# Routed expert blocks: one table built after the last batch, or three tables built after two, three and four batches

## The chip, the cores and the metric

The kernel runs as one program on one core of one Trainium2 chip. The metric is device time in microseconds (us) of one execution; less is better. The core has a matrix engine (PE, with its weight loads PEld), a vector engine (DVE), a scalar engine (ACT), a general engine (POOL), and a queue engine (SP) which here only issues DMAs. Each engine runs its own instructions in a fixed order; engines wait for each other by semaphores.

## The reference, cut to what matters

The input x is 4 batches of 512 tokens of 256 numbers, all fp32. Four layers follow each other. Each adds an attention over a small context (64 keys a batch; layer 1 has a causal self-attention, MLA, besides) and then a feed-forward part. In layers 0, 1 and 3 this part is a mixture of experts, of which each token takes two:

```python
scores = jnp.einsum('btd,de->bte', x, router_w)
probs = softmax(scores)                                   # layer 1: sigmoid
routing_weights, routing_idx = jax.lax.top_k(probs, 2)
routing_weights = routing_weights / jnp.sum(routing_weights, axis=-1, keepdims=True)
gate = einsum(x, gate_proj[expert]);  up = einsum(x, up_proj[expert])
expert_out = (silu(gate) * up) @ down_proj[expert]
y = sum over the two chosen experts of routing_weight * expert_out
...
# layer 1: shared = silu(xt @ Wg_s) * (xt @ Wu_s) @ Wd_s is added for every token
```

Layer 0 has 8 experts with a hidden width of 704, layer 1 has 7 of 256 and a shared one, layer 3 has 8 of 512. Layer 2's feed-forward part is dense (FP4 quantized) and plays no part here. The two snippets are shortened: the reference computes all experts and weights them, the kernel only the chosen ones.

## The kernel before

**Tokens and batches.** x stays on the core as 16 tiles of 128 tokens. A batch `g` (0 to 3) is four tiles. Attention runs batch by batch; as soon as a batch has its attention result, its tokens are routed, while PE works on the next batch.

**Routing a batch** is `route` (L1054) in layers 0 and 3 and the second half of `mla_after` (L1260) in layer 1. Its steps: layer norm (statistics on DVE, a square root on ACT, `ln_rs` and `ln_sh` on DVE L337, the normalized rows `xn` on ACT L340), transposes (`ps_xT` L372), the router's scores (`r_lg`), `top2` (L731: two maxima, then weights through an exp), then `Routed.add` (L817). `add` marks the chosen experts (`e_mk`, `e_pm`), has PE count each token's rank within its expert (`ps_rank` L829 and L830, then `e_rank`), and writes each token's row, with its place and weights, into its expert's region of a DRAM tensor `xs` by eight indirect DMAs from POOL (L842). The regions hold 2048 rows an expert and are zero where nothing was written.

**The table.** Only after the last batch does `add` call `table` (L854 to L885). From the counts of all four batches (`ps_cnt` L858) it lists blocks of 128 rows, expert by expert: for each block its expert and its first row in `xs`, as integers in `e_tab`. The number of blocks is fixed at the worst case, `nb` = 39 (8 experts) or 38 (7 experts).

**The blocks.** `blocks` (L1005) walks the table. SP reads an entry into a register (`value`) and issues the loads that depend on it: `weights(b)` (L913) loads the expert's gate and up matrices `e_wgu` (three buffers) and its down matrix `e_wd` (four), three blocks ahead; `tokens(b)` (L925) loads 128 rows `e_x` (five buffers), five blocks ahead. For each block `up` (L933) transposes the rows (`ps_xe` L939, copied to `e_xT` L942 or L945 by DVE), works out the places and weights (`places` L896, small DVE operations), multiplies (`ps_gu` L953), takes silu on ACT (`e_s` L969) and multiplies gate by up on DVE (`e_h` L970). `turn` (L973) transposes the block before (`ps_he` L982, evacuated to `e_hT`), `down` (L990) multiplies it (`ps_de` L995), weights it on ACT (`e_y` L997) and scatters it from POOL into `ys` (L998). The next layer adds the rows of `ys` to x. The heart of the loop:

```python
for b in range(self.nb):
    now = self.up(b, between)          # between() calls turn for the block before
    if last:
        self.down(turned, *last)
    last = now
    next(other, None)                  # a piece of the next layer's preparation, layer 0 only
    self.weights(b + 3)
    self.tokens(b + 5)
```

**What sets the order.** Each engine's order is fixed when the program is built. Attention runs under `in_order(PE)`: PE's order is as the program writes it, and a list scheduler places the rest. Blocks run under `in_order(DVE, SP)`: DVE and SP as written, PE, ACT and POOL by the scheduler. In `xattn` (L632), the attention of layers 0, 1 and 3, generators interleave batches: `new` prepares the next batch, `old` (`rest`) finishes the one before (products `ps_bc`, `ps_cy` L592 and `cy`, projection `ps_p` L607, addition to x, then `after`, which is `route`), and the current one runs its scores and exponentials (`ctx_weights` L544: `ps_cx` L552, `cpr` L558 on ACT). The MLA loop (L1290) walks steps `t` (row maxima `mq` L1147 of `ps_ms`, weights `mpr` from `ps_mx` L1157, sums `ps_mo` L1180) and gives each a piece of `mla_after` of an older batch. `mla_after` starts with `mla_project` (`ps_mn`, `my`, `ps_myT`, `myT`, `ps_mw`, addition to `xl`), then a second norm, scores, `add` and `shared_expert` (L757: `ps_sg` L766, `ps_su`, `ps_sd`). For the last batch a pipelined `mla_project_last` (L1220 to L1258) takes the place of `mla_project`.

**The seams.** At the end of attention in layer 0 (seam 1 in what follows), of the MLA in layer 1 (seam 2) and of attention in layer 3 (seam 3), the last batch has nothing behind it to interleave with.

Of the kernel before, what the change touches and what calls it, by code (L numbers as in the profile page):

```python
# [22 lines left out]
P = 128  # L23
B, S, E = 4, 512, 256
SC = 64
# [163 lines left out]
class Net:  # L189
# [136 lines left out]
    def layernorm(self, g, out):  # L326

# [7 lines left out]
        nc.scalar.activation(sd, mv[:, :, 1], AF.Sqrt, bias=self.eps)  # L335
        rs, sh = self.sm("ln_rs", [P, GT]), self.sm("ln_sh", [P, GT])
# [295 lines left out]
    def xattn(self, query, values, scale, dv, W, bias, before=None, after=None, keys=None):  # L632
# [4 lines left out]
        with self.room("xattn") as pool, self.banks(mm=4, sc=1), ExitStack() as stack:  # L637
# [14 lines left out]
            def rest(st):  # L652
                yield from self.ctx_values(pool, st, dv, W)
                if after:
                    yield from after(st.g)
# [13 lines left out]
            for st in sts:  # L669
# [14 lines left out]
                some(late)  # L684
                self.ctx_weights(pool, st, 0, scale)
# [10 lines left out]
            some(old, nf + 2)  # L696
            some(late)
            some(old)
# [32 lines left out]
    def top2(self, v, n, below, logits, rows):  # L731

        nc = self.nc
# [6 lines left out]
        if logits:  # L740
            d, e = self.sm("t_d", [P, GT]), self.sm("t_e", [P, GT])
            nc.vector.tensor_tensor(d, m2, m1, ALU.subtract)
            nc.scalar.activation(e, d, AF.Exp)
            nc.vector.tensor_scalar(s, e, 1.0, None, ALU.add)
            nc.vector.reciprocal(wt[:, :, 0], s)
            nc.vector.tensor_tensor(wt[:, :, 1], e, wt[:, :, 0], ALU.mult)
        else:
            r = self.sm("t_r", [P, GT])
            nc.vector.tensor_tensor(s, m1, m2, ALU.add)
            nc.vector.reciprocal(r, s)  # L750
            nc.vector.tensor_tensor(wt[:, :, 0], m1, r, ALU.mult)
            nc.vector.tensor_tensor(wt[:, :, 1], m2, r, ALU.mult)
        return oh1, oh2
# [32 lines left out]
class Routed:  # L786
# [7 lines left out]

    def __init__(self, net, n, F, gu, d, name, stamp, w=None):
        self.net, self.nc, self.n, self.F, self.w = net, net.nc, n, F, w
        self.nf = (F + P - 1) // P
        self.nb = (2 * NT * P + n * (P - 1)) // P
        self.dram_gu, self.dram_d, self.name, self.stamp = gu, d, name, stamp
        self.scattered, self.put, self.loaded = [], [], {}  # L800
        self.run = self.keep("run_", [P, n])
        self.nc.vector.memset(self.run, 0.0)
# [14 lines left out]
    def add(self, g, rows, oh1, oh2):  # L817
# [4 lines left out]
        nc.vector.tensor_copy(pm[:, 0], self.run)  # L822
        for i in range(1, GT):
            nc.vector.tensor_tensor(pm[:, i], pm[:, i - 1], mk[:, i - 1], ALU.add)
        run = self.keep(f"run{g}", [P, n])
        nc.vector.tensor_tensor(run, pm[:, GT - 1], mk[:, GT - 1], ALU.add)
        self.run = run
        ps = net.acc.tile([P, GT, n], F32, tag="acc", name="ps_rank")
        nc.tensor.matmul(ps, net.cst[:, C_LT : C_LT + P], mk, start=True, stop=False)  # L829
        nc.tensor.matmul(ps, net.cst[:, C_ONE : C_ONE + P], pm, start=False, stop=True)  # L830
        rank = net.sm("e_rank", [P, GT, n])
# [19 lines left out]
        if g == B - 1:  # L851
            self.table()

    def table(self):  # L854

        nc, net, n, nb = self.nc, self.net, self.n, self.nb
        ps = net.acc.tile([P, n], F32, tag="acc", name="ps_cnt")
        nc.tensor.matmul(ps, net.cst[:, C_ONE : C_ONE + P], self.run, start=True, stop=True)  # L858
        up, b = net.keep_i("e_up", [P, n]), net.keep_i("e_b", [P, n])
        nc.vector.tensor_scalar(up, ps, float(P - 1), None, ALU.add)  # L860
        nc.vector.tensor_scalar(b, up, 7, None, ALU.logical_shift_right)
        nbf, cum = net.sm("e_nbf", [P, n]), net.sm("e_cum", [P, n])
        nc.vector.tensor_copy(nbf, b)
        nc.vector.tensor_tensor_scan(cum, net.cst[:, C_ONE : C_ONE + n], nbf, 0.0, ALU.mult, ALU.add)
        iota = net.cst[:, C_IOTA : C_IOTA + nb]
        m = n - 1
        wide = [P, nb, m]
        le = self.keep("e_le", wide)
        cb = cum[:, None, :m].to_broadcast(wide)
        nc.vector.tensor_tensor(le, cb, iota[:, :, None].to_broadcast(wide), ALU.is_le)  # L870
        eb, fb, j = net.sm("e_eb", [P, nb]), net.sm("e_fb", [P, nb]), net.sm("e_j", [P, nb])
        nc.vector.tensor_reduce(eb, le, AX.X, ALU.add)
        nc.vector.tensor_tensor(le, le, cb, ALU.mult)
        nc.vector.tensor_reduce(fb, le, AX.X, ALU.max)
        nc.vector.tensor_tensor(j, iota, fb, ALU.subtract)


        nc.vector.tensor_scalar(j, j, float(CAP // P), float(P), ALU.min, ALU.mult)
        tab = self.keep("e_tab", [P, 2, nb], I32)
        nc.vector.tensor_copy(tab[:, 0], eb)  # L880
        nc.vector.scalar_tensor_tensor(tab[:, 1], eb, float(CAP), j, ALU.mult, ALU.add)

        self.eb = self.keep("e_ebs", [P, nb])
        nc.vector.tensor_scalar(self.eb, eb, -float(SC), None, ALU.add)
        self.tab = tab[:1]  # L885

    def value(self, tab, engine, top):
# [5 lines left out]
            skip_runtime_bounds_check_because="the table counts comparisons with n - 1 sums, and clamps the row",  # L893
        )

    def places(self, xb, b):  # L896
# [3 lines left out]
        one, eb = xb[:, R_ONE : R_ONE + 1], self.eb[:, b : b + 1]  # L900
# [12 lines left out]
    def weights(self, b):  # L913
# [3 lines left out]
        pool, sync = self.pool, self.nc.sync  # L917
        es = self.value(self.tab[:, 0, b : b + 1], SP, self.n - 1)
# [86 lines left out]
    def blocks(self, pool, other=()):  # L1005
# [8 lines left out]
        for b in range(3):  # L1014
            self.tokens(b)
# [689 lines left out]
```

## Time and profile before

| | |
|---|---|
| time, median of 3 runs | 2027.19 us (2026.67 to 2031.56) |
| the profiled execution | 2026.92 us |
| its span, first to last instruction | 2025.2 us |
| its mean granted TensorE clock | 0.919 of full speed |
| busy: PE, DVE, ACT, POOL | 1719.9, 974.2, 667.5, 423.5 us |
| DMA: moved, mean rate over the span | 271.59 MB, 134 GB/s |
| one load of `e_wgu`: layer 0, 3, 1 | 1408 KB in 6.1 us, 1024 KB in 5.1, 512 KB in 4.1 |
| one load of `e_x` | 130 KB in 4.8 us |

The busy rows are sums over the whole span. A sum cannot tell where an engine waited, so the page's 40 slices come next, and then stretches of the trace given by start and end in us from the span's start. In a timeline, a row is: start, duration, engine, line, operation, output and inputs, shapes, count, and in brackets how long the engine was idle before it and what ended the wait.

### The profile page before, as it was taken

The numbers are of one execution on the slowest core, as the hardware profiler recorded it, in microseconds if no ns is written. First come the engines' busy times: TensorE is split into PE (matmuls) and PEld (weight loads), VectorE is DVE, ScalarE is ACT, GpSimd is POOL, SyncE is SP. The second block draws the span as 40 slices with busy tenths as digits, with TensorE's granted clock in tenths as the row PEclk, the third lists the DMA queues.
The fourth block names the chain that finished last, engine by engine and source line by source line (L and its number), as shares of the span: only waits on it lengthen the run. The fifth ranks groups of instructions, "written<-read, shape, count | busy, mean of one in ns | idle before, by whom it ended". The sixth has DMA issues, their size and how long they took to land.

```text
span 2025.2 us, 25644 instructions
## 1 busy us (share of the span) xinstructions
PE 1719.9 (85%) x8740; PEld 980.1 (48%) x8740; DVE 974.2 (48%) x2778; ACT 667.5 (33%) x1253; POOL 423.5 (21%) x594
## 2 busy tenths in 40 slices
PE   6875999999869878898999979985998887599994
PEld 3433666666535333343444344444665443355662
DVE  3543344444454334444454335446899454333333
ACT  3431322222253332336343422233455343122221
POOL 2123011111150011122231222223113112311112
PEclk8986999999979988999999889995899898699997
DMA  9615887778320000000000018772000001598995
GB/s 294 180 38 203 319 294 282 288 284 285 133 71 1 16 23 1 1 1 22 1 22 1 22 42 302 265 246 83 1 0 1 12 6 37 186 311 301 302 315 171
DMA packets 109347, 271.59 MB, mean 134 GB/s; under 512 B 13408, under 2 KB 71200, under 8 KB 99104
## 3 DMA queue, kind: packets, MB, share of 16 engines
q1 hardware_dynamic: 82976, 227.97, 33.0%
q0 software_dynamic: 10176, 28.00, 3.7%
q10 hardware_dynamic: 16064, 13.98, 2.1%
q8 instruction: 70, 1.15, 0.2%
q14 instruction: 61, 0.50, 0.1%
HBM read 220.48 MB, written 49.42 MB: 133 GB/s over the span
## 4 chain that ended last, share of the span: by engine, by line
PE 64%; DVE 14%; ACT 5%; issue 3%; POOL 3%; DMA 2%; SPq 0%; ACTq 0%; DVEq 0%; POOLq 0%
PE ps_gu L953 20%; PE ps_de L995 9%; PE ps_ms L1142 4%; PE ps_mo L1180 3%; DVE mq L1147 2%; PE ps_he L982 2%; PE ps_mx L1157 2%; PE ps_f L1564 2%; PE ps_p L607 2%; POOL xs L842 2%; PE ps_bc L586 1%; PE ps_ms L1145 1%; PE ps_xe L939 1%; PE ps_xT L372 1%; PE ps_cy L592 1%
## 5 line engine op out<-in xcount | busy, mean ns | idle before, releaser
L953 PE MATMUL ps_gu<-e_wgu,e_xT 128*128 128x352 f32 (+1 forms) x1088 | 417.7, 524 | 4.4 <-DVE e_xT L945 0.8
L953 PEld LDWEIGHTS ps_gu<-e_wgu,e_xT 128*128 128x128 f32 x1088 | 197.2, 191 | 143.3 <-issue 73.6
L995 PE MATMUL ps_de<-e_wd,e_hT 128*128 128x256 f32 x932 | 232.3, 385 | 3.8 <-ACT e_hT L303 1.5
L970 DVE TENSOR_TENSOR e_h<-e_s,ps_gu 128x352 f32<-128x352 f32 (+2 forms) x155 | 83.5, 539 | 295.0 <-PE ps_gu L953 227.0
L998 POOL DMA_INDIRECT ys<-e_y,e_to x116 | 112.9, 973 | 521.1 <-ACT e_y L997 398.2
L995 PEld LDWEIGHTS ps_de<-e_wd,e_hT 128*128 128x128 f32 x932 | 172.1, 189 | 79.5 <-issue 41.8
L969 ACT ACTIVATE e_s<-ps_gu 128x352 f32<-128x352 f32 (+2 forms) x155 | 74.1, 478 | 326.6 <-PE ps_gu L953 326.6
L1147 DVE TENSOR_REDUCE mq<-ps_ms 128x2 f32<-128x256 f32 (+3 forms) x128 | 105.7, 826 | 139.8 <-PE ps_ms L1145 139.5
L997 ACT ACTIVATE e_y<-ps_de,e_wt 128x256 f32<-128x256 f32 x116 | 55.0, 475 | 259.5 <-PE ps_de L995 248.2
L1159 ACT ACTIVATE mpr<-ps_mx 128x1024 f32<-128x1024 f32 (+3 forms) x128 | 90.1, 704 | 140.1 <-PE ps_mx L1157 136.1
L1142 PE MATMUL ps_ms<-mkT,mqT 32*128 32x512 f32 (+3 forms) x512 | 112.5, 518 | 22.3 <-DVE mq L1147 21.2
L842 POOL DMA_INDIRECT xs<-xn,e_at x96 | 94.1, 981 | 135.2 <-DVE ln_rs L337 75.7
L1157 PE MATMUL ps_mx<-mqm,mkT 32*128 32x128 f32 (+3 forms) x512 | 107.6, 497 | 1.1 <-ACT mpr L1159 1.1
L1161 POOL TENSOR_SCALAR_AFFINE_SELECT mpr<-mpr 128x256 f32<-128x256 f32 x128 | 52.0, 409 | 242.3 <-ACT mpr L1159 242.3
L1180 PE MATMUL ps_mo<-mpr,va 128*32 128x128 f32 (+3 forms) x512 | 96.9, 460 | 3.1 <-POOL mpr L1161 3.1
L1564 PE MATMUL ps_f<-w,xqT 128*128 128x352 f32 x256 | 86.4, 480 | 1.2 <-ACT xqT L1555 1.2
L372 PE MATMUL ps_xT<-consts_sb,xn 128*128 128x128 f32 x256 | 51.8, 341 | 41.8 <-ACT xn L340 27.0
L982 PE MATMUL ps_he<-consts_sb,e_h 128*128 128x128 f32 x466 | 76.2, 278 | 12.0 <-DVE e_h L970 7.9
L939 PE MATMUL ps_xe<-consts_sb,e_x 128*128 128x128 f32 x232 | 51.4, 292 | 37.0 <-DMA e_x<-xs 34.1
L942 DVE COPY e_xT<-ps_xe 128x256 f32<-128x256 f32 x78 | 33.0, 423 | 98.4 <-PE ps_xe L939 98.4
L1142 PEld LDWEIGHTS ps_ms<-mkT,mqT 32*128 32x128 f32 x512 | 41.4, 197 | 77.6 <-DVE mq L1147 52.6
L552 PE MATMUL ps_cx<-q,kbd 32*128 32x512 f32 x256 | 44.0, 786 | 39.5 <-ACT cpr L558 39.5
(314 smaller groups left out, 2776.8 us busy)
## 6 DMA issues: line engine op xcount, KB each, us to landing
e_wgu<-in_e0gu SPq DMA_DIRECT2D x39, 1408.0 KB, 6.1
e_wgu<-in_e3gu SPq DMA_DIRECT2D x39, 1024.0 KB, 5.1
e_wd<-in_e0d SPq DMA_DIRECT2D x39, 768.0 KB, 5.7
e_wd<-in_e3d SPq DMA_DIRECT2D x39, 512.0 KB, 5.4
e_wgu<-in_e1gu SPq DMA_DIRECT2D x38, 512.0 KB, 4.1
xs<-z SPq DMA_DIRECT2D x16, 1040.0 KB, 14.3
e_x<-xs SPq DMA_DIRECT2D x116, 130.0 KB, 4.8
e_wd<-in_e1d SPq DMA_DIRECT2D x38, 256.0 KB, 4.2
```

Source lines behind the costliest of these rows:

```text
L842: r = nc.gpsimd.indirect_dma_start(out=net.xs, out_offset=bass.IndirectOffsetOnAxis(ap=at[:, k, i : i + 1], axis=0), in_=rows[:, i], in_of ...
L953: nc.tensor.matmul(ps[:, :n], xT[:, c], wgu[:, c, cols], start=(c == 0), stop=(c == NC - 1))
L970: nc.vector.tensor_tensor(h[:, k * H : (k + 1) * H], s, u, ALU.mult)
L982: self.nc.tensor.transpose(ps[:r, f - f0], h[:, f * P : f * P + r], net.ident)
L995: nc.tensor.matmul(po[:, :E], hT[:r, f], wd[:r, f], start=(f == 0), stop=(f == self.nf - 1))
L998: r = nc.gpsimd.indirect_dma_start(out=net.ys, out_offset=bass.IndirectOffsetOnAxis(ap=at, axis=0), in_=y, in_offset=None)
L1142: nc.tensor.matmul(ps[:, r, :n], st.qT[o][rows, diag], st.kT[o][rows, :n], start=True, stop=False)
L1147: nc.vector.tensor_reduce(st.q[:, i, at : at + 2, HD], ps[:, :, :n], AX.X, ALU.max, negate=True)
L1157: nc.tensor.matmul(ps[:, r, :n], st.kT[o][rows, keys], st.qm[o][rows, j * P :], start=True, stop=True)
L1159: nc.scalar.activation(pr[:, :, :n], ps[:, :, :n], AF.Exp, scale=HD**-0.5)
L1180: nc.tensor.matmul(st.po[32 * n : 32 * n + 32, j * P :], st.va[:, j, at : at + 32], pr[:, r, : S - j * P], start=(j == 0), stop=(j == GT - 1),
L1564: nc.tensor.matmul(ps[:, :H], xT[:, c], w[:, c, k * H : (k + 1) * H], start=(c == 0), stop=(c == NC - 1))
```

## The change

The table is built in three parts: `table(1)` after batch 1, `table(2)` after batch 2, `table(3)` after batch 3. `cuts` says which blocks each part lists: [0, 9, 17, 39] for 8 experts, [0, 10, 18, 38] for 7. These are the numbers of full blocks (128 rows of one expert) that two and three batches must have whatever the routing is. The first two parts list only full blocks; `taken` remembers which were listed, and the last part lists what is left. `begin`, which is called during attention's last batch (in the MLA, when the third batch's sums end), issues the first three `e_wgu` and five `e_x` loads. The last batch's routing is no longer run by attention: it is handed to `blocks` as a generator, which advances it by one step between the pieces of a block (`per` steps a block, the first of them in `between`: 1 in layers 0 and 3, 3 in layer 1). It must be through before the loads of the third part's entries, so what is left of it is run at block 12 (13). In layer 1 this generator is `mla_after` of the last batch, with `mla_project`, the norm, the scores and the shared expert; `mla_project_last` is removed. `top2` returns its last operations as `weigh`, which `add` runs after the rank products. The pools of memory are rearranged so that `e_wgu` and `e_x` have room during attention.

```diff
-    def add(self, g, rows, oh1, oh2):
+    def add(self, g, rows, oh1, oh2, weigh):
...
-        self.run = run
+        nc.vector.tensor_tensor(self.runs[:, g + 1], pm[:, GT - 1], mk[:, GT - 1], ALU.add)
...
+        weigh()
+        yield
...
-        if g == B - 1:
-            self.table()
+        yield
+        if g:
+            self.table(g)
+        yield
...
+    def table(self, g):
+        nc, net, n, k = self.nc, self.net, self.n, g + 1
+        ps = net.acc.tile([P, k, n], F32, tag="acc", name="ps_cnt")
+        nc.tensor.matmul(ps, net.cst[:, C_ONE : C_ONE + P], self.runs[:, 1 : k + 1], start=True, stop=True)
...
+        nc.vector.tensor_tensor(first, till[:, :k], self.taken[:, :k], ALU.add)
+        if g < B - 1:
...
+            nc.vector.tensor_tensor(till, till, full[:, None].to_broadcast([P, k + 1, n]), ALU.min)
+        nc.vector.tensor_tensor(count, till[:, 1:], till[:, :k], ALU.subtract)
+        nc.vector.tensor_tensor(count, count, self.taken[:, :k], ALU.subtract)
...
+        b0, b1 = self.cuts[g - 1 : g + 1]
...
+        self.listed(first, count, cum, b0, b1)
...
+    def listed(self, first, count, cum, b0, b1):
...
+        for at in range(0, nb, 512 // q):
+            part = slice(at, min(nb, at + 512 // q))
+            wide = [P, part.stop - at, q]
+            le = net.acc.tile(wide, F32, tag="acc", name="ps_le")
+            nc.vector.tensor_tensor(
+                le, cum[:, None, 1 : q + 1].to_broadcast(wide), iota[:, part, None].to_broadcast(wide), ALU.is_le
+            )
+            nc.vector.tensor_tensor(le, le, step[:, None].to_broadcast(wide), ALU.mult)
+            nc.vector.tensor_reduce(row[:, part], le, AX.X, ALU.add)
...
+        self.tables.append((b0, tab, eb))
...
-    def blocks(self, pool, other=()):
+    def begin(self, pool):
+        self.held, self.xb, self.wgu, self.wd = pool, {}, {}, {}
+        self.weights(0, (True, False))
+        for b in range(3):
+            self.tokens(b)
+        for b in range(1, 3):
+            self.weights(b, (True, False))
+            self.tokens(b + 2)
+
+    def blocks(self, pool, routing, per=1, other=()):
...
-        self.weights(0)
-        for b in range(3):
-            self.tokens(b)
-        for b in range(1, 3):
-            self.weights(b)
-            self.tokens(b + 2)
+        for b in range(3):
+            self.weights(b, (False, True))
...
             turned = last and self.turn(last[1])
+            next(routing, None)
...
             last = now
+            for _ in range(per - 1):
+                next(routing, None)
             next(other, None)
+            if b + 5 == self.cuts[-2]:
+                for _ in routing:
+                    pass
             self.weights(b + 3)
             self.tokens(b + 5)
...
             def rest(st):
                 yield from self.ctx_values(pool, st, dv, W)
-                if after:
+                if after and st.g < B - 1:
                     yield from after(st.g)
...
                 some(late)
+                if st.g == B - 1:
+                    begin()
                 self.ctx_weights(pool, st, 0, scale)
...
-            old = rest(sts[-1])
-            some(old, nf + 2)
+            for _ in old:
+                some(late, 1)
             some(late)
-            some(old)
...
-    def mla_project_last(self, pool, st):
...
-        yield from (self.mla_project if g < B - 1 else self.mla_project_last)(pool, st)
+        yield from self.mla_project(pool, st)
...
+            if last == (B - 2, 3, GT - 1, 1):
+                soon()
...
-        behind(-1)
+        while len(old) > 1:
+            behind(1)
+        return old[0]
...
-            moe.blocks(pool)
+                moe.blocks(pool, last, 3)
...
+                        moe.blocks(pool, self.route(moe, B - 1, self.rw0, fine=True), other=later())
...
+                moe.blocks(pool, self.route(moe, B - 1, self.rw3, fine=True))
```

## The prediction

> **What bounds the kernel now.** I read the page's busy shares first (PE 85% of 2025.2 us), then the slices, which show three dips of PE at the seams between attention and expert blocks, then the table by stage over those seams (columns: stage, length, busy us of PE, PEld, DVE, ACT, POOL, granted clock, DMA share, GB/s):
>
> ```profile
> 156.00:190.00 34.00, 9.55 (x40) 7.71 (x39) 11.60 (x64) 5.73 (x9) 15.70 (x16) 0.57 0.42 143
> 1175.00:1216.00 41.00, 29.25 (x108) 19.16 (x107) 17.75 (x70) 9.28 (x20) 10.80 (x12) 0.79 0.17 55
> 1726.00:1758.00 32.00, 9.06 (x38) 7.21 (x37) 11.00 (x60) 5.73 (x9) 15.69 (x16) 0.58 0.38 128
> 190.00:555.00 365.00, 352.43 (x1440) 237.48 (x1439) 157.77 (x519) 90.10 (x220) 50.32 (x62) 1.00 0.75 274
> ```
>
> The blocks (last row) keep PE 97% busy at full clock; seams 1 and 3 use PE for 28% at little over half clock. The timeline of PE in seam 1 says what it waits for, and that of seam 2 why that one is cheaper:
>
> ```profile
> 156.05 0.39 PE L830 MATMUL ps_rank<-e_pm,consts_sb 128*128 128x32 f32 x2
> 159.85 0.33 PE L372 MATMUL ps_xT<-consts_sb,xn 128*128 128x128 f32 x1 [3.41 <-ACT xn L340]
> 169.81 0.64 PE L829 MATMUL ps_rank<-e_mk,consts_sb 128*128 128x32 f32 x2 [3.21 <-DVE e_mk L821]
> 170.86 0.57 PE L858 MATMUL ps_cnt<-run,consts_sb 128*128 128x8 f32 x2
> 188.38 0.69 PE L939 MATMUL ps_xe<-consts_sb,e_x 128*128 128x128 f32 x2 [16.95 <-DMA e_x<-xs]
> 189.72 5.84 PE L953 MATMUL ps_gu<-e_wgu,e_xT 128*128 128x352 f32 x16
> ...
> 1188.18 1.18 PE L372 MATMUL ps_xT<-consts_sb,xn 128*128 128x128 f32 x4 [3.72 <-DVE xn L363]
> 1200.03 3.78 PE L766 MATMUL ps_sg<-xnT,sgu 128*128 128x512 f32 x4
> 1214.81 0.44 PE L939 MATMUL ps_xe<-consts_sb,e_x 128*128 128x128 f32 x2 [0.89 <-DMA e_x<-xs]
> ```
>
> A chain of one: layernorm of batch 3, top two, rank, eight scatters on POOL (10 us), their landing, the token load; 16.95 us of it PE sees as one DMA wait. In seam 2 the shared expert (1200 to 1214) already covers scatter and load.
>
> **Part 1: the blocks start early.** The compiled order of the changed kernel puts weight and token loads of the first blocks on SP before the last batch's routing, waiting only for batch 1's scatters, so the e_x wait goes at seams 1 and 3. Three e_wgu and five e_x loads move there, past nothing but each other: SP has no other work then, and DMA is 7 to 11% busy. The e_wd loads stay behind, when attention's memory is free, about 164 in seam 1; three of 768 KB take 8 us at the blocks' 274 GB/s, and the first ps_de comes 12 us after the first ps_gu (201.65 against 189.72), so they cost 0; with e_wgu in their way they would cost a block's load, 5 us. What is late next is DVE. The same order puts table(1) (22 DVE operations) among batch 2's layernorm, ahead of ln_rs, and table(2) (about 27) ahead of the second cy product, on which ps_p and so block 0 wait. The second group of ps_cx waits for an exp that stands behind that layernorm on ACT:
>
> ```profile
> 129.51 0.18 DVE L337 RECIPROCAL ln_rs<-ln_sd 128x4 f32<-128x4 f32 x1 [0.36 <-ACT ln_sd L335]
> 132.06 1.28 ACT L558 ACT_TABLE_LOAD   x1
> 133.35 1.88 ACT L558 ACTIVATE cpr<-ps_cx 128x2048 f32<-128x2048 f32 x1
> 135.28 1.24 PE L552 MATMUL ps_cx<-q,kbd 32*128 32x512 f32 x4 [6.14 <-ACT cpr L558]
> ...
> 1736.76 0.19 DVE L706 TENSOR_REDUCE t_m<-r_lg 128x4 f32<-128x32 f32 x1
> 1736.98 0.19 DVE L708 TENSOR_TENSOR t_eq<-r_lg,t_m 128x32 f32<-128x32 f32 x1
> ...
> 172.91 0.45 DVE L870 TENSOR_TENSOR e_le<-e_cum,consts_sb 128x273 f32<-128x273 f32 x1
> ```
>
> Small dependent DVE operations follow each other every 0.22 us, two interleaved chains every 0.11; wide compares take about 0.15 + 1.1 ns per element (228 wide 0.40, 273 wide 0.45). The old table never showed a PSUM destination or width 512; I take this slope for both, 0.71 us for 512.
> - table(1): between e_rank and ln_sh the trace has 2.3 us (127.62 to 129.88); with the table's operations among them 5.35. The exp and PE move by 3.1 us.
> - table(2): e_rank to the second cy takes 6.3 us. In the trace that cy ends 152.73 (seam 1). Now r_lg comes 3.1 later, e_mk at 153.3, e_rank at 154.85 (1.5 after e_mk, as at 169.56 to 171.09), cy ends at 161.0: 8.3 late.
> - Block 0's e_xT stands on DVE behind the last x add (156.94 + 8.3 = 165.2), so its first ps_gu starts near 165.7 instead of 189.72: 24.0 won. Seam 3 by the same steps: 1735.7 instead of 1758.23, 22.5, and 1.5 since its first block runs warm (5.35 us for eight ps_gu, 3.67 in steady blocks): 24.
>
> **Part 2: the last batch's routing runs inside blocks** (seams 1 and 3). PE does its xT, r, rank and cnt anyway: 1.9 + 1.95 + 0.7 + 0.35 = 4.9 at full clock. DVE runs a written order in the blocks, so a step delays the e_h and e_xT behind it, for which PE waits. A block of 8.9 us (seam 1; 6.2 in seam 3) has about 4.3 (3.3) us of DVE. Layernorm statistics (2.2), top2 (2.6), marks (1.9) and ranks (1.6) fit its gaps: 1.0 (0.6) charged. table(3) does not: 18 dependent operations at 0.22, 0.3 more, and 3 x 0.71 + 3 x 0.36: 7.6 us in one block. In seam 1 it would start after the evacuation that ends at 210.27 and end at 217.9; e_h till 218.4, one reduction of w_gate 0.4, so e_xT starts at 218.9 instead of 214.4 (behind the ps_xe of 213.96): PE loses 4.5. In seam 3, counted from e_xT: places till 1.3, evacuation 2.0, table 9.6, e_h 10.3, ps_he 11.0, where ps_gu would have come at 6.6: 4.4. The scatters hold SP at token load 11 until they land (8 x 1.28 on POOL plus 2.5); the weights behind that load are needed three blocks later, 18 us at least, so it costs 0; without that cover a weight load (5 to 6 us) per seam. y scatters behind them on POOL have six buffers.
>
> Here a rule weighs. The first ps_gu after an idle PE ran 0.75 us (seam 1) and 1.7 (seam 3) longer than warm ones, and eight ps_cx take 1.14 us after work, 2.09 after 6.14 idle. The Trainium skill, "TensorE: Matmul & The Clock Gate", Part 1, says that an idle window of about 3.4 us halves the clock for about 3.4 us. So a stall of 4.5 us costs again: 1.7 by the rule, 1.0 (1.2) by my rows; I take the rows, which would make 1.2 us difference in all. A second: each seam's ACT table loads (sqrt, exp, silu) now fall between silus, with one or two reloads of silu. "ScalarE: Activation LUTs", What ACT_TABLE_LOAD costs, gives 2.66 us a switch with its drain; the load at 132.06 is followed after 1.29 us by its exp, no drain seen. By the trace a round trip of 2.6 us hides; by the rule 5.3 would add about 2 us a seam, 6 in all. The trace decides: 0.
>
> Net seam 1: 24.0 - 4.9 - 4.5 - 1.0 - 1.0 = 12.6. Seam 3: 24.0 - 4.9 - 4.4 - 1.2 - 0.6 = 12.9.
>
> **Part 3: seam 2** has three steps a block. The pipelined last projection is gone; per block the chain ps_gu 1.85, ps_mn 0.6, rs and my 0.8, ps_myT 0.4, myT's copy behind e_h 0.5, ps_mw 1.1, xl and the first e_xT 1.0 (all from 1174.99 to 1179.4 and the blocks at 1225) makes 6.25 us, against 3.51 for a plain block. Four of them 25.0; rmsnorm and xT block 6.5; scores 7.1; marks and ranks 7.1; the table, behind which sg and su run, 10.8; shared expert 8.5 and 4.8: 69.8 us for ten blocks. From ps_gu 0 at 1176.0 block 10 starts at 1245.8; before, 1218.90 + 9 x 3.51 = 1250.5. Won 4.7. table(1) falls among the mq reductions of attention, one bank deep: a burst of 4 us where 1.5 are free costs 2.5; table(2) falls behind the last reduction, hidden by sg and su. Net 2.2.
>
> Sum: 12.6 + 12.9 + 2.2 = 27.7. The profiled execution took 2026.9 (span 2025.2, 1.7 around it), 0.3 below the median of the runs: 1999.
>
> **Rivals.**
> - All hidden. DVE's written order costs nothing and PE's work is the bound: seams 1 and 3 win 24 - 4.9 each; seam 2 has 35 us of blocks and 25 of routing on PE against 75.4 now (1175.1 to 1250.5), less 2.5 for table(1): 12.9. In all 51, 1976. For it: DVE is 43% busy in the blocks. Against: 7.6 us in one piece.
> - Slower. Every step of routing holds DVE at a PE or ACT result not yet there, and e_xT behind it. There are 8 steps in seams 1 and 3 and 30 in seam 2; beyond what I charged it decides from 27.7 / 46 = 0.6 us a step. At 0.9 more a step: 41 lost, 2041. For it: r_lg today waits 3.2 us for ps_r. Against: most steps stand a block behind their producers in the compiled order.
> - It doesn't do what it says: the first loads wait for the last scatters because xs is one tensor. Then gain 0 and the tables on top, 6 us: 2033. Against: the order of their waits on SP.
>
> **How the numbers follow.** Likeliest 1999, within 1985 to 2015, chance 0.55. All hidden or nearly, 1970 to 1985: 0.24. Gain eaten down to the last few us, 2015 to 2033: 0.14. Slower by the step mechanism or an early wait: 0.07. This measurement tells about 0.3%, 6 us, from no change: faster 0.85, same 0.08, slower 0.07. Range 1974 to 2021, with PSUM operations at twice my slope (3 us each in three places) inside it.
>
> **What would show it.** The first ps_gu of the three block stages near 166, 1166 and 1721 (each shifted by what was won before it); e_x off PE's waits in seams 1 and 3; the wait of ps_cx for cpr up from 6 to 9 us; e_tab operations ahead of a PE gap of 4 to 5 us in block 7; seam 2's first ten blocks at 70 us. Wrong if PE waits for e_wgu or e_wd in blocks 8 to 12, if block 7 shows no gap, or if seam 2's blocks run under 5 us from the start.

## The result, and the profile after

The changed kernel takes 1994.77 us (median of 4, 1989.64 to 1997.21) where the kernel before takes 2029.38 in the same session (median of 4): 0.983 of it, 95% interval 0.981 to 0.985. A second session gave 1994.32 (ratio 0.9825, 0.980 to 0.985). 1999 was predicted. The profiled executions are 2026.92 and 1997.21 us, a gain of 29.7 where the sum said 27.7; 1997.21 is the slowest of its four runs, though, and the medians lie 34.6 apart. The second session's profile of the changed kernel ("again" in what follows) took 1993.34. The parts of the gain were not all the predicted ones.

The table by stage of the changed kernel, with the same columns as the one shown of before (seam 1 up to block 0, the first ten blocks of layer 0, seam 2 with its first blocks, seam 3 with its first blocks):

```profile
156.00:172.00 16.00, 12.78 (x47) 7.09 (x47) 11.89 (x54) 4.25 (x6) 7.86 (x8) 0.91 0.79 284
165.30:259.45 94.15, 89.62 (x373) 61.50 (x374) 45.65 (x184) 30.04 (x60) 19.61 (x20) 0.98 0.82 303
1165.00:1250.00 85.00, 71.18 (x284) 41.70 (x282) 47.41 (x203) 23.89 (x53) 22.08 (x25) 0.96 0.50 168
1712.00:1780.00 68.00, 60.33 (x235) 37.60 (x236) 38.63 (x155) 19.71 (x32) 21.41 (x22) 1.00 0.76 257
```

The 34 us in which PE was 28% busy at a clock of 0.57 are gone: block 0 of layer 0 starts at 165.30 instead of 189.72, and the stretch after it has PE 95% busy with the whole routing inside it. The timeline of PE at the end of attention and in the block that holds table(3):

```profile
154.10 0.38 PE L844 MATMUL ps_rank<-e_mk,consts_sb 128*128 128x32 f32 x2 [1.52 <-DVE xn L756]
154.62 0.41 PE L845 MATMUL ps_rank<-e_pm,consts_sb 128*128 128x32 f32 x2
155.12 1.65 PE L591 MATMUL ps_bc<-crs,pairs_sb 128*128 128x512 f32 x2
156.70 1.94 PE L597 MATMUL ps_cy<-cpr,va 128*32 128x512 f32 x8
...
160.71 3.29 PE L612 MATMUL ps_p<-Wo_sb,cy 128*128 128x256 f32 x14 [1.27 <-DVE cy L605]
165.30 4.97 PE L1030 MATMUL ps_gu<-e_wgu,e_xT 128*128 128x352 f32 x16 [1.29 <-issue]
...
237.90 4.51 PE L1072 MATMUL ps_de<-e_wd,e_hT 128*128 128x256 f32 x12 [2.83 <-DVE e_row L938]
242.61 3.72 PE L1030 MATMUL ps_gu<-e_wgu,e_xT 128*128 128x352 f32 x12
```

No wait for e_x is left ahead of ps_gu. One long wait is new: ps_de waits 2.83 us for DVE while DVE builds the table, and the twelve ps_de then take 4.5 us instead of the 2.95 of a warm block. DVE at that place:

```profile
237.15 0.69 DVE L938 TENSOR_REDUCE e_row<-ps_le 128x16 f32<-128x512 f32 x1
240.58 0.52 DVE L1047 TENSOR_TENSOR e_h<-e_s,ps_gu 128x352 f32<-128x352 f32 x1
241.84 0.36 DVE L1019 COPY e_xT<-ps_xe 128x256 f32<-128x256 f32 x1
```

ps_de itself needs nothing of the table: it starts when the reduction of ps_le ends (237.84), and ps_le, the table's scratch, takes its buffers from the same two in PSUM as ps_de (`tag="acc"`). PE would have stood still a little later anyway, since e_h and e_xT are behind the table on DVE until 242.20, and ps_gu begins at 242.61. Note the order of PE's first rows as well: ps_rank stands between the two ps_cy of the last batch.

From stage to stage the 29.7 us come about like this. Blocks are timed by e_y, the last ACT step of each; "layer 1" runs from the last e_y of layer 0 to the last of layer 1. The last column sets "again" against the same profile of before; its sum is 33.6.

| | predicted | measured | again |
|---|---|---|---|
| seam 1: start of block 0 | +24.0 | +24.4, and 0.7 as block 0 runs warm | +22.2, and 0.7 |
| its routing on PE | -4.9 | -0.8 | -0.8 |
| table(3), with the cold clock after it | -5.5 | -4.2 | -4.2 |
| rest | -1.0 | 0 | 0 |
| seam 1 | 12.6 | 20.1 | 17.9 |
| layer 1 | +2.2 | -1.1 | +2.4 |
| layer 2 | 0 | +0.7 | -0.1 |
| seam 3: start of block 0, warm start | +24.0 | +22.2 | +25.7 |
| its routing on PE; table(3) | -4.9; -5.6 | -3.3; -3.3 | -3.3; -3.5 |
| rest | -0.6 | -5.8, all in blocks 22 to 38 | -5.8 |
| seam 3 | 12.9 | 9.9 | 13.2 |

So a row of this table moves by up to 3.5 us between two executions of the same kernel.

### The profile page after: what moved, and what is told of

It reads as the page before. It is cut to its first block, busy times and chain, and to the rows that moved or that the text cites. A ratio compares the mean times of both kernels' runs of the same rounds, so it can differ in the third digit from the quotient of the medians.

```text
span 1995.5 us, 25928 instructions
## 1 busy us (share of the span) xinstructions
PE 1712.2 (86%) x8752; PEld 970.5 (49%) x8752; DVE 1020.4 (51%) x3011; ACT 671.4 (34%) x1254; POOL 424.3 (21%) x594
## 4 chain that ended last, share of the span: by engine, by line
PE 69%; DVE 18%; ACT 6%; issue 3%; DMA 2%; POOL 1%; SPq 0%; ACTq 0%; DVEq 0%; POOLq 0%
PE ps_gu L1030 20%; PE ps_de L1072 10%; PE ps_ms L1235 4%; PE ps_mo L1273 3%; DVE mq L1240 2%; PE ps_p L612 2%; PE ps_mx L1250 2%; PE ps_f L1633 2%; PE ps_xT L377 2%; PE ps_he L1059 2%; PE ps_bc L591 2%; ACT cpr L563 2%; PE ps_cx L557 1%; PE ps_ms L1238 1%; PE ps_cy L597 1%
## 5 line engine op out<-in xcount | busy, mean ns | idle before, releaser
L557 PE MATMUL ps_cx<-q,kbd 32*128 32x512 f32 x256 | 45.2, 806 | 44.1 <-ACT cpr L563 44.1
L1019 DVE COPY e_xT<-ps_xe 128x256 f32<-128x256 f32 x78 | 33.0, 423 | 86.7 <-PE ps_xe L1016 86.7
L1059 PEld LDWEIGHTS ps_he<-consts_sb,e_h 128*128 128x128 f32 x466 | 53.7, 138 | 29.4 <-DVE e_h L1047 13.7
```

What stands on the lines that cost most here:

```text
L1059: self.nc.tensor.transpose(ps[:r, f - f0], h[:, f * P : f * P + r], net.ident)
```

## The experiments

Each changes the changed kernel, unless said otherwise; "changed" below is the profiled execution above. The median of the changed kernel to compare with is 1994.3 to 1994.8, its eight runs 1989.64 to 1997.21. The cuts of code are shortened; what stands in them behind # or between < and > says in words what the edit does.

**1. The table in pieces.**

```diff
-            self.table(g)
+            for _ in self.table(g):      # table and listed now yield in four places
+                if g == B - 1:
+                    yield
```

> Only table(3) is cut into five pieces, one a step, so that one block holds 1 to 2 us of its DVE operations instead of 7.6. Theory (the written order of DVE makes one long piece, which holds up e_h and PE behind it): the block of layer 0 that took 13.9 us falls to 9 to 10, the 2.8 us wait of ps_de for e_row goes, and the 1.6 + 1.6 us gaps of layer 3 go; 4 to 5 us won in seam 1, 2.5 to 3.3 in seam 3, 0 to 2 in layer 1, so a span of 1986 to 1989 against 1995.5. Rival (DVE is short of time in these blocks as a whole): five blocks lose about 1 us each in place of one that loses 5, and the span stays at 1994 to 1996.

Measured: 1980.59 us (ratio 0.977, 0.974 to 0.980), 14 less; span 1979.7. From first ps_gu to the last e_y layer 0 takes 360.3 us instead of 364.4, as much as before the change (360.1); layer 3 loses 3.2 less in its first blocks (69.5 instead of 72.7). The block that took 13.88 us takes 8.89, and PE no longer waits:

```profile
233.88 1.35 PE L1037 MATMUL ps_gu<-e_wgu,e_xT 128*128 128x352 f32 x4
235.07 2.95 PE L1079 MATMUL ps_de<-e_wd,e_hT 128*128 128x256 f32 x12
237.95 0.44 PE L1023 MATMUL ps_xe<-consts_sb,e_x 128*128 128x128 f32 x2
```

So the stall came of the table in one piece, not of DVE's load, and it could be had back whole: 4.1 and 3.2 us. The pieces free two things at once, DVE for e_h and e_xT, and the PSUM buffers that ps_le shares with ps_de; which of them counted was not separated. In layer 1 they gain nothing (177.1 us from the last ps_mo to the last e_y, changed 176.3). In its profile a further 11.8 us lie in the MLA (423.4 instead of 435.3), where nothing was edited; experiment 3 is about that. So of the 14 us between the medians the pieces account for 7.3 only.

**2. The MLA's entry: memory, then fills.** In the changed kernel the first ps_ms comes 171.6 us after layer 1's first ps_cx, before it 163.8. Of these 7.8 us, 4.2 lie between the last ps_p and ps_lat (9.8 against 5.6 us), and 3.4 between ps_lat and ps_ms. The timeline of DVE in the first of these stretches, changed:

```profile
702.68 1.01 DVE L364 TENSOR_SCALAR rms_e<-rms_n 128x4 f32<-128x4 f32 x1
703.94 4.33 DVE L368 TENSOR_SCALAR xn<-xl,rms_r 128x256 f32<-128x256 f32 x4
```

Before, the same two rows take 0.16 and 1.14. POOL's nine fills of q, k and values run from 700.8 to 708.1 here, over both rows; before, one ran at 603 and the others at 696 to 699 and 716 to 719. First their memory was exchanged:

```diff
+        for g in (1, 2):                 # ahead of the first q and k
+            sts[g].va = short.tile(...)
```

> Only the memory of two MLA value tiles (va1, va2) and of the first q and k is exchanged, so that the first memset on POOL no longer waits for the last ps_p of layer 1's cross-attention. Theory (POOL's memsets run beside DVE's four xn operations and slow them, 4.3 us for four against 1.1 before the change): memsets start several us before the last ps_p ends, the four xn take 1.1 to 1.5 us, ps_lat comes 3 to 5 us earlier after the last ps_p; span 1990 to 1992. Rival (xn is slow for another reason, its operands or where its rows lie): xn stays above 3 us, span within 1 us of 1995.5.

The edit missed: the first fill still waited for the last ps_p (705.46), xn took 4.32. What its 1989.14 us (0.981), some 5 less than the changed kernel, come from is open; its profile has the MLA at 423.5 us. Then five of the fills were moved:

```diff
-                nc.gpsimd.memset(st.va, 1.0)
+            nc.gpsimd.tensor_scalar(st.va, <first mkT, broadcast>, 0.0, 1.0, ALU.mult, ALU.add)
...
+        # likewise q and k of batch 1: they cannot start before batch 0's keys are transposed
```

> Only five of POOL's eight fills at the MLA's entry (second q and k, second and third values) are put behind the first transposed keys of batch 0. Theory (fills on POOL slow DVE's xn beside them): the four xn take 1.1 to 2 us instead of 4.3, rms_e 0.2 instead of 1.0, the stretch from the last ps_p to the first ps_ms is 3 to 4 us shorter than 39.0. Rival (the first three fills alone do it, or the late ones hold up the rotated keys instead): no more than 1 us shorter. Outside that stretch nothing changes; span 1981 to 1993, as the MLA's clock windows fall.

Measured: 1994.71 us (0.982), the same. DVE and POOL in it:

```profile
707.17 1.01 DVE L364 TENSOR_SCALAR rms_e<-rms_n 128x4 f32<-128x4 f32 x1
708.42 1.14 DVE L368 TENSOR_SCALAR xn<-xl,rms_r 128x256 f32<-128x256 f32 x4
```

```profile
707.10 1.05 POOL L1366 MEMSET va<- 128x1148 f32 x1
708.09 0.23 POOL L1352 MEMSET mk<- 128x64 f32 x1
```

rms_e, still beside a fill, takes 1.01; xn, begun after the last fill, takes 1.14 again. So a fill on POOL does hold up such a DVE operation: that half of the theory stands. ps_lat came 3.3 us sooner after ps_p, but the time did not follow: the median is the same. In the profile the next stretch, from ps_lat to the first ps_ms, is as long as changed has it (22.0 us), while "again" has 18.27: PE had a lower clock in it (0.73 granted on average over 711.7 to 733.7, against 0.95 over 715.6 to 733.8 of "again"). Of ten executions with the same instructions there, five have 22.0 and five 18.2 to 19.1, so these 3.7 us are no effect of an edit, and a gain of 3.3 is too small to be told from four runs that span 8 us.

**3. The same kernel once more.**

> The changed kernel itself once more, to see its MLA. Theory (the 435 us from the first ps_ms to the last ps_mo were one execution's clock windows, 61.3 us at half clock; kernels with the same instructions there took 423 to 424 with 44.3 us at half clock): 423 to 425 us now, span 1983 to 1987. Rival (something in this kernel's own order makes it): 434 to 436 again, span 1994 to 1997.

Measured: 1994.32 us, span 1991.6. The MLA, first ps_ms to last ps_mo, took 430.8 us, between the two expectations. All kernels with the same instructions there, in one profiled execution each: 435.3 (changed), 430.8, 423.4 (experiment 1), 423.5, 423.2, 430.5, 423.4, 428.9, 427.1, 423.2. Whole-stage rows of the changed kernel, then of experiment 2's first kernel:

```profile
732.00:1168.00 436.00, 387.16 (x2406) 166.64 (x2408) 194.28 (x424) 170.04 (x280) 96.73 (x194) 0.93 0.04 13
```

```profile
733.00:1157.00 424.00, 378.73 (x2404) 165.44 (x2408) 194.62 (x423) 169.91 (x280) 96.59 (x194) 0.95 0.04 14
```

DVE, ACT and POOL are busy for the same time; PE is busy 8.4 us longer over the same matmuls, at a mean clock of 0.93 against 0.95. By the trace's records of the granted clock, the five executions with 423 to 424 us each had half clock for 44.4 us of this stage, the other five for 51.2 to 61.3. So most of the MLA's 7.6 us in the changed profile is not the change: the mean of the ten is 426.9, before it was 427.7. The tables of batches 1 and 2 cost the MLA nothing that can be told from this. The Trainium skill, "TensorE: Matmul & The Clock Gate", Part 1, says that the clock gate's window of about 3.4 us is free-running, so the same kernel meets it in a different phase from run to run; that fits these rows, though no run here steered the phase.

**4. Layer 1 as it was before.**

```diff
-            with self.in_order(PE):
-                last = self.mla(pool, short, tail, moe, sgu, sd, soon)
+            # one room, mla_project_last, one table after batch 3, begin() at the blocks
```

> Layer 1 as before the change (one table after the last batch, the pipelined last projection, the old memory), layers 0 and 3 as changed. Theory (in layer 1 the change gives back in the MLA what it wins at the seam): first ps_ms 5 to 6 us earlier, the MLA loop 7 us shorter, the stretch from the MLA's last ps_mo to block 10 six us longer, the later blocks 6 us longer; span within 3 us of 1995.5. Rival (the changed seam 2 is worth its price, since the MLA's losses come from layer 0's change): the MLA keeps its losses and the span is 2003 to 2009.

Measured: 2001.11 us (0.986, 0.984 to 0.989), 6.5 more than the changed kernel: neither expectation's size. Layer 1 takes 824.1 us, of which the stretch to the first ps_ms is 5.0 shorter (166.6), the MLA 430.6, the stretch from the last ps_mo to block 9 86.7 instead of 74.9, the later blocks 108.5 instead of 101.7. So the change does win at seam 2 and in the later blocks; it gives back part at the entry only. The kernel before needs 80.3 for the stretch that takes 86.7 here: its first ps_gu comes 3.5 us later after the last ps_mo, with the new, longer table on the path, and its first blocks take 3.9 us instead of 3.51. So some 6 of its us are the variant's own, and against before the change wins 5.4 at seam 2.

**5. PE's order in layer 3's blocks.** In the last 17 blocks before the change and in all of the changed kernel's, by the timeline of PE (before, then changed):

```profile
1906.28 3.60 PE L953 MATMUL ps_gu<-e_wgu,e_xT 128*128 128x512 f32 x8
1909.71 1.89 PE L995 MATMUL ps_de<-e_wd,e_hT 128*128 128x256 f32 x8
1911.44 0.60 PE L982 MATMUL ps_he<-consts_sb,e_h 128*128 128x128 f32 x4
1911.88 0.38 PE L939 MATMUL ps_xe<-consts_sb,e_x 128*128 128x128 f32 x2
1912.10 3.60 PE L953 MATMUL ps_gu<-e_wgu,e_xT 128*128 128x512 f32 x8
```

```profile
1883.73 3.67 PE L1030 MATMUL ps_gu<-e_wgu,e_xT 128*128 128x512 f32 x8
1887.24 1.89 PE L1072 MATMUL ps_de<-e_wd,e_hT 128*128 128x256 f32 x8
1888.97 0.38 PE L1016 MATMUL ps_xe<-consts_sb,e_x 128*128 128x128 f32 x2
1889.19 0.60 PE L1059 MATMUL ps_he<-consts_sb,e_h 128*128 128x128 f32 x4
1889.87 3.70 PE L1030 MATMUL ps_gu<-e_wgu,e_xT 128*128 128x512 f32 x8
```

In the first, ps_gu starts 0.22 us after ps_xe, too soon to be using it: that ps_xe is the next block's. In the second, ps_xe is the block's own, and ps_gu starts 0.68 us after ps_he, where the four ps_he need 0.44: the other 0.24 PE waits until DVE has copied ps_xe. 5.82 against 6.17 us a block; the list scheduler chose the first for before's last blocks only. The edit makes it the written order:

```diff
             turned = last and self.turn(last[1])
+            if ahead and n < self.nb:
+                self.lifted[n] = self.lift(n, self.xb[n])    # ps_xe of the next block
...
-                with self.in_order(DVE, SP):
+                with self.in_order(PE, DVE, SP):             # layer 3 only
```

> Only layer 3's blocks: PE's order is also as written, with the transposes ps_xe of a block one block earlier (after ps_he, ahead of the second half of ps_gu). Theory (the two cadences of 6.17 and 5.82 us a block come from whether ps_xe stands one block ahead on PE, so that ps_gu does not wait for e_xT): 5.8 us a block throughout, 10 to 13 us won in layer 3, span 1983 to 1986. Rival (6.17 is set by the weight loads, 1.67 MB a block at some 290 GB/s): the cadence stays at 6.1 or more, with waits of ps_gu for e_wgu, span 1994 to 1997.

Measured: 1984.73 us (0.979, 0.976 to 0.982), 10 less. All steady blocks take 5.82; blocks 9 to 38 take 165.9 us instead of 176.0. In the first blocks the fixed order of PE costs 4.7: PE waits 1.4 us ahead of ps_xT, 1.0 ahead of ps_rank and 2.8 once ahead of ps_de. So layer 3 gains 5.4 us net, about half of what was expected; the rest between the medians is not this edit's as far as the profile shows (its MLA took 423.2). The loads are not the limit of these blocks.

**6. Layer 0 without its own side work.**

```diff
-            next(other, None)
+            if b >= 9:
+                next(other, None)
```

> Only layer 0's preparation of the next layer (the work that blocks advance by one piece a block) starts nine blocks later. Theory (the last batch's transposes and scores cost seam 1 almost nothing, because they fall into holes that this preparation makes on PE, where ps_he waits 1.5 us for e_hT): with the preparation away, routing shows its price, the first six blocks take 8.9 us plus the 1.0, 1.9 and 0.7 us of xT, r and rank, about 3.6 in all above 8.9 each, and the two holes of 1.5 to 1.9 us come back after block 9, so layer 0 takes 3 to 4 us more than in the changed kernel. Rival (routing on PE is free for another reason): the first six blocks stay at 8.9 us, holes come later, and layer 0 takes the same within 1 us.

Measured: 2011.55 us (0.992, 0.989 to 0.995). The mechanism shows, the total was missed. Blocks 1 to 5 take 9.94, 10.33, 8.89, 9.50, 8.89, so routing costs PE 3.1 us where 3.6 was expected, and two holes of 2.45 return at blocks 11 and 13. But from first ps_gu to last e_y layer 0 takes 365.7 us against 364.4, only 1.3 longer: the first ten blocks are 1.9 shorter without the side work, the rest 3.1 longer. And the last nine pieces of side work are left over and run after the blocks (the first ps_cx of layer 1 comes 45.2 us after the last e_y instead of 30.8), which was in no expectation. Changed, then before, what fills the hole:

```profile
190.11 0.60 PE L1059 MATMUL ps_he<-consts_sb,e_h 128*128 128x128 f32 x4
190.55 1.85 PE L733 MATMUL ps_r<-router_w_sb,xnT 128*128 128x8 f32 x16
192.26 0.44 PE L1059 MATMUL ps_he<-consts_sb,e_h 128*128 128x128 f32 x2
```

```profile
214.17 0.60 PE L982 MATMUL ps_he<-consts_sb,e_h 128*128 128x128 f32 x4
216.32 0.44 PE L982 MATMUL ps_he<-consts_sb,e_h 128*128 128x128 f32 x2 [1.54 <-ACT e_hT L303]
```

**7. The first loads when the blocks begin** (layers 0 and 3).

```diff
-                        lambda: moe.begin(held), ...
+                        moe.begin(pool)      # inside the block stage, in its own memory
```

> In layers 0 and 3 the first weight and token loads are issued when the blocks begin, into memory that attention still uses, with the tables in parts and the routing inside the blocks as changed; layer 1 as changed. Theory (the early table lets the loads land under attention, and without that cover the first block pays a load of 6.1 us in layer 0 and 5.1 in layer 3 after attention's memory is free): first ps_gu 5 to 8 us later at each of the two seams, waits of ps_xe or ps_gu for e_x or e_wgu there, 10 to 15 us in all, median 2004 to 2010. Rival (the first loads find free memory or the last x additions set the start anyway): first ps_gu within 1 us of the changed kernel's, median 1993 to 1996.

Measured: 2002.76 us (0.986, 0.983 to 0.990), 8 more. The first ps_gu comes 138.9 us after the first ps_cx in layer 0 (changed 130.0, again 131.7), 136.7 in layer 3 (133.6, 130.2), behind this wait in layer 0:

```profile
170.72 0.69 PE L1016 MATMUL ps_xe<-consts_sb,e_x 128*128 128x128 f32 x2 [6.98 <-DMA e_x<-xs]
```

The theory's mechanism holds; the sum falls short of it, as the first ps_cx comes at 33.1 instead of 35.3: room held for the early loads costs 2.2 us at the start of layer 0. In the changed kernel PE waits 3.02 us there for xnT ahead of ps_q (0.9 here), and ps_q takes 6.61 us where before has 5.17.

**8. table(2) out of attention**, in layers 0 and 3; `add` leaves it out there.

```diff
+    def last_route(self, moe, rw):
+        moe.table(2)
+        yield
+        yield from self.route(moe, B - 1, rw, fine=True)
```

> In layers 0 and 3 table(2) is built in the first block, in one piece, instead of during attention's last batch; all else as changed. Theory (table(2)'s 27 DVE operations stand before the second cy product and delay the first block by some 5 us, the larger part of the 8.3 charged): first ps_gu 4 to 5.5 us earlier at both seams (160 to 163 in layer 0), and a stall of 2 to 4 us in the first two blocks, net 1 to 3 us a seam, median 1989 to 1993. Rival (what delays the second cy is the wait for ranks and top two, and table(2) rides beside it): first ps_gu no more than 1 us earlier, the stall in block 0 or 1 on top, median 1995 to 2000.

Measured: 1998.73 us (0.985, 0.983 to 0.988). The theory's 4 us or more are not there: the first ps_gu comes 131.0 us after the first ps_cx in layer 0, where nine executions with the changed kernel's attention have 129.8 to 132.2, and 128.3 in layer 3, 1.9 under the 130.0 to 130.3 of six of them (three have 133.0 to 133.6). table(2) in one piece in block 0 costs 10.7 us in layer 0 and 3.7 in layer 3. The second cy on DVE in layer 0, changed, then here:

```profile
159.83 0.23 DVE L940 TENSOR_SCALAR e_row<-e_row,e_base 128x8 f32<-128x8 f32 x1
159.97 0.69 DVE L605 TENSOR_TENSOR cy<-ps_cy,cbs 128x512 f32<-128x512 f32 x1
```

```profile
159.91 0.69 DVE L605 TENSOR_TENSOR cy<-ps_cy,cbs 128x512 f32<-128x512 f32 x1 [2.89 <-PE ps_cy L597]
```

In the changed kernel ps_cy is done at 158.64, and cy stands behind the table until 159.97: table(2) does hold it up, by 1.3 us. Here cy waits for PE alone, and PE is later, at a granted clock of 0.50 over 151.0 to 160.6 (changed 0.82). So the run does not say that table(2) is worth nothing; it says that PE's part of the wait is as long.

**9. The order at the end of attention.**

```diff
-            for _ in old:
-                some(late, 1)
+            some(old)
             some(late)
```

> As the kernel with table(2) in the first block, and besides, at the end of attention in layers 0, 1 and 3, PE's written order is again that of before the change: both ps_cy products of the last batch, then ps_p, then the ranks of batch 2 (the change had put each routing step of batch 2 between two pieces of the last batch, ps_rank between the two ps_cy). Theory (on PE in written order the second ps_bc and ps_cy stand behind ps_rank, which waits for the top two: that, not table(2), is what delays block 0): the second cy comes 2.5 us after the first or sooner instead of 6.4, the first ps_gu 2.5 to 4 us earlier than without this edit (125 to 128.5 us after the first ps_cx, against 131.0), the blocks as before this edit; median 1992 to 1996. Rival (the second cy waits for its operands anyway): no more than 1 us earlier, median 1997 to 2000.

Measured, beside experiment 8: first ps_gu after 127.4 and 124.9 us, 3.6 and 3.4 sooner; 1995.01 us (0.983), 3.7 less. PE in it:

```profile
153.18 1.66 PE L597 MATMUL ps_cy<-cpr,va 128*32 128x512 f32 x8
154.77 1.12 PE L591 MATMUL ps_bc<-crs,pairs_sb 128*128 128x512 f32 x2
155.82 1.07 PE L597 MATMUL ps_cy<-cpr,va 128*32 128x512 f32 x8
...
160.90 0.30 PE L844 MATMUL ps_rank<-e_mk,consts_sb 128*128 128x32 f32 x2
162.41 5.00 PE L1030 MATMUL ps_gu<-e_wgu,e_xT 128*128 128x352 f32 x16 [0.98 <-DVE e_xT L1019]
```

The second cy comes 2.05 us after the first, against 6.4 in experiment 8 and 7.25 in the changed kernel. It stood behind ps_rank on PE, which waited for the top two. That holds with table(2) out of the way; PE's old order with table(2) left in attention was not run.

**10. Together.** The table in pieces, ps_xe a block ahead in all three layers with PE's order left to the scheduler, late fills:

> Together: table(3) in five pieces, ps_xe written one block earlier in all three layers with PE's order left to the scheduler, five fills late. If the effects add: 4 us in seam 1 and 3 in seam 3 from the pieces, 10 in layer 3 and 0 to 6 in layer 1 from ps_xe, 3 from the fills: median 1968 to 1976. Rival (ps_xe takes the transposes' PSUM from ps_he, two buffers for both, and in layer 0 with its two groups of ps_he PE waits): layer 0's blocks become slower than 8.9 to 9.2 us, median 1978 to 1990.

Measured: 1963.93 us (0.965, 0.960 to 0.971; runs from 1947.84 to 1969.25), 30 less than the changed kernel and under the expected sum. From block 11 on layer 0 takes 8.68 to 9.05 us a block, where the changed kernel takes 8.89 to 9.44; with the pieces it is 15.2 us shorter in all, of which only 4 had been expected. Layer 3 takes 5.82 a block and is 12.9 shorter. The same with table(2) in three pieces in the first blocks instead of the late fills:

> Together: table(3) in five pieces, table(2) in three pieces inside the first blocks, ps_xe one block earlier in all three layers. If table(2) is worth 4 to 5 us a seam when it is spread: median 1954 to 1959, against 1963.9 of the same without it. If it isn't: 1963 to 1968.

Measured: 1964.04 us (0.969, 0.967 to 0.972), no better: block 0 starts 2 to 5 us sooner, but the blocks take 6.5 us more in layer 0 and 4.1 more in layer 3.

## Why the prediction was right, step by step

The seams, the early loads, the new start and the stall of table(3) were read rightly, and PE waits for no e_wgu or e_wd in the first blocks. That the two profiles came out within 2 us of the sum is luck: seam 1 gave 7.5 us more than was said, layer 1 and seam 3 together 6.3 less. In "again" layer 1 and seam 3 come as predicted, only seam 1 is 5.3 above, and the gain is 33.6; the medians say 34.6 and 35.2. So the sum was 6 to 7 us too small, well within its range.

- **Start of block 0.** 165.7 was derived and 165.30 measured (167.48 in "again"), the second cy until 161.0 derived and 160.66 measured. The agreement is in part luck, as the delay of this cy has other parts than the prediction's 3.1 and 5.2. Of the 7.9 us measured, 2.6 are a later first ps_cx (35.29 instead of 32.73; experiment 7), for which there was no term. table(1) delayed the exp as said, but less: ps_cx waits 8.42 us for cpr instead of 6.14, and counted from the first ps_cx that group comes 1.4 later, where 3.1 was charged. The other 4.0 lie between it and the second cy. They were put on table(2) alone, but two waits stand side by side there: DVE's behind table(2), and PE's behind ps_rank, which the written order has ahead of ps_cy. Experiment 8 took the first away and won 0 to 1.9 us; experiment 9 took the second away as well and won 3.5. The compiled order was read on DVE and SP and not on PE.
- **Routing on PE.** "PE does its xT, r, rank and cnt anyway: 4.9" was the mis-sized term of seam 1. Measured: 0.8, since ps_r fell into a hole of 1.54 us that PE had there for layer 0's side work; 3.1 without that (experiment 6) and 3.3 in layer 3. PE at 97% over 365 us hid that its first five blocks had holes.
- **table(3).** 7.6 us of DVE were estimated (the terms as written add up to 7.5); it ran from 233.68 to 240.68, 7.0, in block 6 and not 7, with the 512-wide operations on PSUM at 0.69 to 0.70 (the slope had said 0.71). It cost PE 4.2 and 3.3 net, where 5.5 and 5.6 were charged: the block after made up 0.8, and in layer 3 the two waits of 1.59 left the clock at full. That ps_le takes PSUM buffers from ps_de was not in the prediction; in layer 0 it moved the wait ahead of ps_de. After the 2.83 us wait in layer 0 the twelve ps_de lost 1.5, between the trace's 1.0 and the rule's 1.7.
- **Seam 2.** Ten blocks in 70.3 us, 69.8 derived. But "before, 1218.90 + 9 x 3.51" was wrong: from its seventh block on, before takes 3.95, by another order of PE. The changed kernel keeps 3.51 until block 24, which won 6.9 us that no step had. Against it stand the MLA's entry and the MLA itself. The entry had no term, as the edit of the rooms was costed at nothing: 7.8 us in this profile, 3.1 to 10.4 in ten executions of the same instructions, of which 4.2 are the fills beside DVE (experiment 4, with the old memory, has before's 5.6 us from ps_p to ps_lat). The MLA, charged 2.5, lay in these ten between 4.5 us below and 7.6 above before's one.
- **Seam 3.** The late blocks' cadence, 5.82 before and 6.17 after, was taken to be the same: 5.8 us. Experiment 5 shows that PE's order makes it.
- **The rivals.** "All hidden" (1976) did not happen; table(3) in pieces comes nearer to it, at 1980.6, though only 7.3 us of that are accounted for. The slower way did not: steps of routing stood far enough behind their producers, 3.3 us for all that layer 3's routing cost outside the table.
- **The ACT loads** among the silus: with six table loads of ACT between 165 and 235 us, PE's waits for ACT from 165 to 300 add up to 1.4 us, against 3.6 from 189 to 300 before. Block 3, with one of the loads in it, took the plain 8.89. No cost shows, as taken from the trace.
- **Two readings without effect.** DMA was read as 7 to 11% busy during the last batches of attention; from 130 to 156 us it is 17%, from 1640 to 1700 us 5%. Three e_wd loads take 8.6 us at 274 GB/s, not 8. Neither bears on the sum.

## What to carry to other kernels

Starting a stage early by splitting a table wins the length of the idle seam; what it gives back lies where the moved work stands in one long piece on an engine with a written order, so cut such work into pieces from the start. Read the compiled order on every engine, above all on the one that runs in written order: the same delay had two waits behind it, and DVE's order alone showed only one. Compare steady cadences of before and after over the whole loop, not over its first blocks: the scheduler's choice for one transpose moved as much time here as the change's own costs. And take the terms of a sum from more than one execution of each kernel before calling them right or wrong.

## What was not expected of the hardware

- A POOL fill beside DVE's tensor-scalar operations on SBUF (fp32) slows them from 0.285 to 1.08 us each (128x256), one with four elements from 0.16 to 1.01; x additions (0.76) and a reciprocal (0.18) beside the same fills kept their times. The Trainium skill, "SBUF — State Buffer", section "SBUF: two separate sides", says that DVE in a 2-port mode and POOL exclude each other on a shared pair of ports for a whole instruction; a fill takes 0.95 to 1.2 us, so the rows agree, though none of them says in which mode DVE ran.
- Ten executions of the same MLA instructions took 423.2 to 435.3 us, for the most part by their clock: a difference of one to ten us between two single profiles, in a stage that waits often for short times, is no finding.
- The half clock comes in stretches of whole multiples of 3.41 us in these traces, all but the last, which the end of the trace cuts off: the MLA's 44.4, 51.2, 54.6 and 61.3 us are 13, 15, 16 and 18 times that. One such stretch (237.5 to 240.9) lies at the end of the wait of 2.83 us and behind it, so the next 4.7 us had 0.68 granted on average; "again" has the same wait and the same stretch. Two waits of 1.59 us were followed by none.
